# One-hot rows of a graph layer built from pairs of 16-bit numbers, in groups of blocks on VectorE

## The chip, the cores and the metric

The kernel runs on one core of a Trainium2 chip. The core has five engines that run side by side and are tied together by semaphores only: PE (TensorE, matmul and transpose, results in PSUM), DVE (VectorE), ACT (ScalarE), POOL (GpSimd) and SP (SyncE, which mainly issues DMAs). The metric is the device time of one execution in microseconds. Before the change it is 753.4 us, the median of three runs (752.56 to 754.88).

## The reference, cut to what matters

There are 1250 nodes with 512 features and 21250 edges (20000 random ones and one loop per node), sorted by target. Two layers follow each other, each on a layer-normalised and rectified input, each added to `x`:

```python
h = max(layernorm(x), 0)
# graph attention
h = h @ W + b_w
e = leaky_relu((h @ a[:512])[dst] + (h @ a[512:])[src] + b_a, 0.2)
w = exp(e)
x += segment_sum(w / segment_sum(w, dst)[dst] * h[src], dst)
# mixture of four experts, each of two graph convolutions; each node uses its best two
h = max(layernorm(x), 0)
gates = softmax(h @ gate_W + gate_b);  top_v, top_i = top_k(gates, 2)
conv(h) = relu(segment_mean(h[src], dst) @ Wl + bl + h @ Wr)
x += sum over the two chosen experts of top_v * conv2(conv1(h))
```

## The kernel before, in words

The edges are turned into a dense matrix of counts, `AT[source, target]`, and both layers use it as a matrix. Nodes lie in `NT` = 10 tiles of `T` = 125, and edges in `NB` = 170 blocks of `EB` = 125, one edge of a block per partition. As the edges are sorted by target, the targets of tile `t` lie in a window of 19 to 23 neighbouring blocks (`window[t]`), and successive windows share about six blocks.

**How the counts arise.** The count matrix of a tile is a sum of matmuls over the blocks of its window: a one-hot row per edge for its target (`hd`) times a one-hot row per edge for its source (`hs`). To count all 1250 sources with one row of 125, the source number is written as `q * 125 + low`. The row has its one at `low`, and the one is replaced by the power of two `4 ** q` (`val`). The sum in PSUM is thus a packed number, of which two bits hold the count for each of the ten source tiles. One more column of ones, at `T`, gives the degree of the target. The packed sum is copied out (`pack`, `deg`), transposed (L374), and its ten digits are cut out by shifts and masks (`digit`, L356 and L359) and cast to `AT` (L421).

`hd` is made by one VectorE comparison per tile (L382): `iota` (16-bit floats, 0 to 1252) against `idx["dst"]` (32-bit floats, one number per edge and block, repeated along 128 columns). `hs` is made block by block into a ring of `RING` = 27 rows in the tile `first`, because the windows overlap and a row can be used by two tiles. Three blocks in four are made by one VectorE instruction (L399: equal to `low`, then times `val`, both as numbers per partition). Each fourth block is made by two ScalarE instructions (L394, L395): the distance from `low`, and `relu(val - val * distance)`. `low`, `val` and `less` (minus `val`) are computed once for all blocks (L304 to L310).

**The stages in order.** First x, W and the indices are loaded, the indices are transposed so that a block's edges lie on partitions (L284), and copied to `idx` (L286). The vector `a` is spread over partitions and W is multiplied with it (L294), so that the projection also gives both attention scores. `project(t)` normalises a tile of x (L178, ScalarE), transposes it (L185), rectifies it into `hT` (L186), multiplies it by W (L333) and adds the bias on VectorE (L335). The statistics that `normalize` needs are made by `norms` in batches: for tiles 0 and 1, for 2 to 4, and for 5 to 9, the last batch when `project(5)` starts. A batch is a bn_stats (L168) and a bn_aggr (L169) per tile, then one square root on ScalarE (L171), one reciprocal (L172) and one product (L174) for all its tiles.

The target tiles form three chunks (tiles 0-3, 4-6 and 7-9). `count(ci)` counts one chunk, `attend(ci)` does its attention: scores on ScalarE (L435, L436), times counts on VectorE (L442), matmul with `hW` on PE (L448), sum of the weights on POOL (L446). `count(0)` is woven into the projections of tiles 2 to 7, `count(1)` into `attend(0)`, and `count(2)` into `attend(1)`. Then come the second normalisation (L491 makes the gate sums), the means over neighbours (L578), and the four experts (from about 235 us on, L854 to L1036), which work on the chosen nodes gathered into slots. `number_slots`, among the means, numbers the slots of each expert: its VectorE comparison L734 makes a one-hot row of 128 for each node, expert and tile (`spots`).

**What sets the order.** The text gives each engine's instructions an order and a priority, but the planner of the tile framework may issue a ready instruction ahead of ones written earlier, so the order in the trace differs from the text: source rows that `count(0)` writes after the second projection stand among the preparations at 15 us. `tc.keep_in_program_order(i)` holds instruction `i` behind the instruction of the same engine that was written last before it. Each engine then runs its queue strictly in order. The pool `hot` has two buffers per tile (`hd`, `xn`, `hT`, `pack`), the pool `small` three, and PSUM eight banks.

## Time and profile before

| | before |
|---|---|
| median of 3 runs | 753.4 us (752.56 to 754.88) |
| the profiled execution | 752.97 us, of which 751.2 us is the span |
| PE busy | 715.0 us (95%) |
| PE weight loads | 580.0 us (77%) |
| DVE busy | 500.0 us (67%) |
| ACT busy | 247.3 us (33%) |
| POOL busy | 164.6 us (22%) |
| mean granted PE clock | 0.987 |

The span is the time from the first to the last instruction. "Busy" is the time in which an engine has at least one instruction under way; the ends of matmuls are modelled, so a busy PE need not be at its peak. A line of the timeline or of the groups names an engine, a line of the code, the operation, and the tiles as output<-input. In brackets or behind a bar stands how long the engine was idle just before, and whose result ended the idle time. A share of busy time over the whole span says little here, since the stages have different limits: the experts take two thirds of the span, and the changed lines all lie in the first third.

### The profile page before, as it was taken

Reading aid. Unit: us, or ns where it says so; the run is one execution under the profiler, and the core shown is the slowest. Engines: PE = TensorE matmul, PEld = TensorE weight load, DVE = VectorE, ACT = ScalarE, POOL = GpSimd, SP = SyncE. Lnnn points to the kernel's source line nnn. Section 1 sums busy time; section 2 is a strip of 40 time slices with the busy share of each in tenths; the row PEclk is TensorE's granted clock in tenths of the full one; section 3 lists DMA queues with packets and bytes.
Section 4 is the critical chain, followed back from the end, with each engine's and each line's share of the span. In section 5 each row is a group of like instructions: output and inputs, shape, how many; then the busy total and the mean of one; then the engine's idle time right before and its main releaser. Section 6 shows DMA issues by size and latency. Waiting matters only on the chain. (4 is left out here: it accounts for less than half of the span.)

```text
span 751.2 us, 9943 instructions
## 1 busy us (share of the span) xinstructions
PE 715.0 (95%) x3409; PEld 580.0 (77%) x3409; DVE 500.0 (67%) x1321; ACT 247.3 (33%) x565; POOL 164.6 (22%) x151
## 2 busy tenths in 40 slices
PE   7969999998999999899999999999999999999993
PEld 4757545545998888788888888888888888887883
DVE  6898899699887569356964554568364554557642
ACT  4648957872200012111222333103031333104320
POOL 1101544231002002020132321300232321400431
PEclk9989999999999999999999999999999999999997
DMA  8000001101307312181133223721132322601332
GB/s 213 8 8 4 4 8 58 43 7 42 118 23 188 119 55 72 44 283 42 56 99 56 35 47 57 228 97 44 54 80 47 49 38 51 186 28 57 81 64 30
DMA packets 30636, 52.95 MB, mean 70 GB/s; under 512 B 7305, under 2 KB 8755, under 8 KB 30568
## 3 DMA queue, kind: packets, MB, share of 16 engines
q0 software_dynamic: 6848, 15.77, 11.3%
q1 hardware_dynamic: 15570, 20.44, 9.2%
q10 hardware_dynamic: 8150, 15.90, 6.2%
q8 instruction: 34, 0.56, 0.3%
q14 instruction: 34, 0.28, 0.1%
HBM read 33.55 MB, written 19.20 MB: 70 GB/s over the span
## 5 line engine op out<-in xcount | busy, mean ns | idle before, releaser
L448 PE MATMUL p_o<-hW,P 125*125 125x512 f32 x200 | 91.4, 598 | 1.8 <-DVE P L442 1.6
L960 PE MATMUL p_s<-h_hi,AS 125*128 125x512 f32 x210 | 83.8, 399 | 1.1 <-DVE v L932 1.1
L117 ACT ACTIVATE h_hi<-v 125x512 fp32r<-125x512 f32 x40 | 24.9, 629 | 178.8 <-DVE v L929 141.2
L960 PE MATMUL p_s<-h_lo,AS 125*128 125x512 f32 x210 | 81.8, 389 | 0.0
L864 PE MATMUL p<-T,S 128*125 128x256 f32 x320 | 73.9, 382 | 0.4 <-DVE v L913 0.2
L864 PEld LDWEIGHTS p<-T,S 128*125 128x125 f32 x320 | 60.3, 189 | 11.0 <-DVE v L913 2.0
L966 DVE TENSOR_SCALAR agg<-p_s,asel 128x512 f32<-128x512 f32 x22 | 16.5, 750 | 76.2 <-PE p_f L854 39.4
L841 ACT CAST AS<-digs 125x256 fp32r<-125x256 int32 x150 | 54.8, 403 | 36.9 <-DVE digs L356 31.4
L846 POOL DMA_INDIRECT hsel<-h,reads x32 | 36.3, 1136 | 133.2 <-DMA h<-v 54.0
L448 PEld LDWEIGHTS p_o<-hW,P 125*125 125x125 f32 x200 | 35.3, 188 | 37.4 <-issue 34.6
L972 POOL DMA_INDIRECT out_dram<-y,writes x22 | 35.4, 1608 | 130.9 <-ACT y L1008 59.0
L446 POOL TENSOR_TENSOR den<-den,P 125x375 f32<-125x375 f32 (+1 forms) x27 | 40.2, 1490 | 46.5 <-DVE P L442 42.1
L356 DVE TENSOR_SCALAR digs<-packed 125x128 int32<-125x128 int32 x279 | 45.6, 219 | 3.0 <-ACT packed L835 2.2
L960 PEld LDWEIGHTS p_s<-h_hi,AS 125*128 125x128 f32 x210 | 39.4, 188 | 9.6 <-issue 1.4
L856 ACT ACTIVATE gT<-p_f 128x512 f32<-128x512 f32 x22 | 13.5, 616 | 99.8 <-PE p_f L854 99.8
L960 PEld LDWEIGHTS p_s<-h_lo,AS 125*128 125x128 f32 x210 | 39.5, 188 | 8.0
L827 POOL DMA_INDIRECT asel<-packs,reads x35 | 36.5, 1043 | 33.2 <-DVE agg L966 19.4
L333 PE MATMUL p_h<-W_sb,hT 128*125 128x257 f32 (+1 forms) x160 | 40.6, 408 | 2.9 <-ACT hT L186 2.8
L578 PE MATMUL p_ag<-AT,h_hi 125*128 125x416 f32 (+1 forms) x120 | 42.6, 355 | 0.0
L864 PE MATMUL p<-wr,h2T 128*125 128x256 f32 x160 | 39.3, 390 | 3.4 <-DVEq L1071 2.3
L578 PE MATMUL p_ag<-AT,h_lo 125*128 125x416 f32 (+1 forms) x120 | 42.2, 352 | 0.0
L399 DVE TENSOR_SCALAR first<-iota,low,val 125x125 bf16<-125x125 f16 x128 | 39.4, 378 | 1.9 <-PE p_a L403 1.9
(239 smaller groups left out, 1443.5 us busy)
## 6 DMA issues: line engine op xcount, KB each, us to landing
h<-v SPq DMA_DIRECT2D x40, 224.0 KB
wl<-in_L_gnn_Wl_dram ACTq DMA_DIRECT2D x7, 1024.0 KB
wr<-in_L_gnn_Wr_dram ACTq DMA_DIRECT2D x7, 1024.0 KB
out_dram<-x SPq DMA_DIRECT2D x10, 224.0 KB
x<-in_x_dram SPq DMA_DIRECT2D x1, 1120.0 KB
h<-v SPq DMA_DIRECT2D x40, 26.0 KB
W_sb<-in_L_gnn_W_dram SPq DMA_DIRECT2D x4, 256.0 KB
wl<-in_L_gnn_Wl_dram SPq DMA_DIRECT2D x1, 1024.0 KB
```

Of the source, the lines that this page charges most:

```text
L333: nc.tensor.matmul(p[:T, :n], hT[:, k, :], W_sb[:, k, half, :n], start=(k == 0), stop=(k == KF - 1))
L356: nc.vector.tensor_scalar(o, v, BITS * d, (1 << BITS) - 1, op0=OP.logical_shift_right, op1=OP.bitwise_and)
L399: nc.vector.tensor_scalar(hs[:, :T], iota[:EB, :T], low[:, j:j + 1], val[:, j:j + 1], op0=OP.is_equal, op1=OP.mult)
L446: nc.gpsimd.tensor_add(den[:, :n], den[:, :n], P[:, :n])
L448: nc.tensor.matmul(po[i][:T, :], P[:, i * T:(i + 1) * T], hW[:, s - 1, :, :HD], start=(s == 1), stop=(s == NT))
L578: nc.tensor.matmul(p[:, :n], h2[s][i][:, m * 128:(m + 1) * 128], AT[:, s, c], start=(s == 0 and i == 0), stop=(s == NT - 1 and i == 1))
L827: nc.gpsimd.indirect_dma_start(a, None, packs, bass.IndirectOffsetOnAxis(reads[:, j:j + 1], 0))
L841: nc.scalar.copy(AS[:, d:d + 2, :], dig)
L846: nc.gpsimd.indirect_dma_start(r, None, h1, bass.IndirectOffsetOnAxis(reads[:, j:j + 1], 0))
L864: nc.tensor.matmul(p, A[:, k, :], B[:, k, :], start=(i == 0 and k == 0), stop=(i * KF + k == n - 1))
L960: nc.tensor.matmul(p, A[:, s, :], hs[s][f], start=(s == order[0] and f == 0), stop=(s == order[-1] and f == 1))
L972: s = nc.gpsimd.indirect_dma_start(out, bass.IndirectOffsetOnAxis(writes[:, j:j + 1], 0), y, None, bounds_check=N - 1, oob_is_err=False, c ...
```

## The change

The diff does five things.

1. **Targets.** `idx["dst"]` becomes a 16-bit float with every number written twice (`twice`), and the comparison for `hd` views 128 columns as 64 pairs (`by_two`): the repeated operand now has two equal adjacent 16-bit numbers in its innermost dimension, where it had one 32-bit number with a step of zero.
2. **Sources.** `low` (16-bit float) and `val` (bfloat16) are also written twice. `source_rows` makes up to eight blocks at once by two VectorE instructions: a comparison with `low` into the ring and a multiplication by `val` in place. A group ends where the ring or the tile's window ends. The two ScalarE instructions per fourth block, `far` and `less` are gone. A row is `HOT` = 126 wide, the column of ones stands at 126, and the ring's rows are 128 numbers apart instead of 126.
3. **Preparation.** The power of two is made in `power`, and copied to the bfloat16 pairs. `idx["src"]` and `power` live in the pool that is released after the first projection.
4. **Statistics.** The batch for tiles 5 to 9 is written right after the first `hd` (`next(counts0)`) instead of at the start of `project(5)`, and each of its bn_aggr is held in program order.
5. **Spots.** The comparison of L734 works on pairs as well, from a 16-bit copy of `at` with every number twice.

The diff, without the context that says nothing more:

```diff
@@ -158,7 +158,7 @@
     AT = adj.tile([T, NT, N], F32R, name="AT")
     AT32 = AT.bitcast(F32)
-    def norms(tiles):
+    def norms(tiles, in_order=False):
         n = len(tiles)
@@ -166,7 +166,9 @@
         for i, xt in enumerate(tiles):
             st = small.tile([T, 6], F32, name="st")
             nc.vector.bn_stats(st, xt)
-            nc.vector.bn_aggr(mv[:, i, :], st)
+            last = nc.vector.bn_aggr(mv[:, i, :], st)
+            if in_order:
+                tc.keep_in_program_order(last)
         rs = small.tile([T, NT], F32, name="rs")
         nc.scalar.activation(rs[:, :n], mv[:, :n, 1], AF.Sqrt, bias=eps[:T, :])
         nc.vector.reciprocal(rs[:, :n], rs[:, :n])
@@ -225,9 +227,10 @@
     load_x(5, NT)
     first = feat.tile([128, KF * N], F32, name="first", tag="first")
-    SW = T + 1
+    HOT = T + 1
+    SW = HOT + 1
     RING = max(hi - lo + 1 for lo, hi in window) + 4
-    spare = first[:, RING * SW // 2:]
+    spare = first[:, RING * 64:]
     a_line = spare[:1, :2 * D]
     nc.scalar.dma_start(a_line, rows_of(a, 1, 2 * D))
@@ -243,8 +246,8 @@
     iota = build.tile([128, NI], F16, name="iota")
     nc.gpsimd.iota(iota, pattern=[[1, NI]], base=0, channel_multiplier=0,
                    allow_small_or_imprecise_dtypes=True)
-    ring = first[:, :RING * SW // 2].bitcast(BF16).rearrange("p (r n) -> p r n", r=RING)
-    nc.gpsimd.memset(ring[:, :, T:], 1.0)
+    ring = first[:, :RING * 64].bitcast(BF16).rearrange("p (r n) -> p r n", r=RING)
+    nc.gpsimd.memset(ring[:, :, HOT:], 1.0)
@@ -274,6 +277,13 @@
     a_b = [spread(a_line[:, h * D:(h + 1) * D], D) for h in range(2)]
+    def twice(name, dtype):
+        return build.tile([EB, NB, 2], dtype, name=name)
+    def by_two(v):
+        return v.rearrange("p r (a b) -> p r a b", b=2)
     idx = {}
     for name in ("dst", "src"):
@@ -282,9 +292,14 @@
         p = bank("p_i")
         for c in range(2):
             nc.tensor.transpose(p[:EB, c * NH:(c + 1) * NH], f[:, c, :], ident[:NH, :NH])
-        i = build.tile([EB, NB], F32, name=f"i_{name}")
-        nc.scalar.copy(i.rearrange("p (j c) -> p c j", c=2),
-                       p[:EB, :NB].rearrange("p (c j) -> p c j", c=2))
+        pv = p[:EB, :NB].rearrange("p (c j) -> p c j", c=2)
+        if name == "dst":
+            i = twice("i_dst", F16)
+            nc.scalar.copy(i.rearrange("p (j c) b -> p c j b", c=2),
+                           pv[:, :, :, None].to_broadcast([EB, 2, NH, 2]))
+        else:
+            i = prep.tile([EB, NB], F32, name="i_src")
+            nc.scalar.copy(i.rearrange("p (j c) -> p c j", c=2), pv)
         idx[name] = i
     xnorms = norms(xs[:2])
@@ -296,18 +311,17 @@
                 op0=OP.mult, op1=OP.mult, accum_out=W_sb[:, k, half, HD:]))
     xnorms += norms(xs[2:5])
-    low = build.tile([EB, NB], F32, name="low")
-    val = build.tile([EB, NB], I32, name="val")
-    less = build.tile([EB, NB], F32, name="less")
+    low, val = twice("low", F16), twice("val", BF16)
+    power = prep.tile([EB, NB], I32, name="power")
     q = prep.tile([EB, NB], F32, name="q")
     shift = 0.5 - 0.5 / T
     nc.vector.tensor_scalar(q, idx["src"], 1.0 / T, -shift, op0=OP.mult, op1=OP.add)
     nc.vector.tensor_scalar(q, q, ROUND, -ROUND, op0=OP.add, op1=OP.add)
-    nc.vector.scalar_tensor_tensor(low, q, float(-T), idx["src"], op0=OP.mult, op1=OP.add)
-    nc.vector.tensor_scalar(val, q, float(BITS), 127.0, op0=OP.mult, op1=OP.add)
-    nc.vector.tensor_scalar(val, val, 23, None, op0=OP.logical_shift_left)
-    val = val.bitcast(F32)
-    nc.vector.tensor_scalar(less, val, -1.0, None, op0=OP.mult)
+    nc.vector.scalar_tensor_tensor(low, q[:, :, None].to_broadcast([EB, NB, 2]), float(-T),
+                                   idx["src"][:, :, None].to_broadcast([EB, NB, 2]), op0=OP.mult, op1=OP.add)
+    nc.vector.tensor_scalar(power, q, float(BITS), 127.0, op0=OP.mult, op1=OP.add)
+    nc.vector.tensor_scalar(power, power, 23, None, op0=OP.logical_shift_left)
+    nc.vector.tensor_copy(val, power.bitcast(F32)[:, :, None].to_broadcast([EB, NB, 2]))
     for half in range(2):
         junk = prep.tile([128, 2, HD], F32, name="junk")
         nc.vector.scalar_tensor_tensor(junk, bw_b[:, :, :HD], 1.0,
@@ -318,8 +332,6 @@
     def project(t):
-        if t == 5:
-            xnorms.extend(norms(xs[5:NT]))
         xn = hot.tile([T, D], F32, name="xn")
         normalize(xn, xs[t], xnorms[t])
         hT = hot.tile([128, KF, T], F32, name="hT")
@@ -358,7 +370,20 @@
         else:
             nc.vector.tensor_scalar(o, v, BITS * d, None, op0=OP.logical_shift_right)
-    made = set()
+    made = [0]
+    GROUP = 8
+    def source_rows(until):
+        while made[0] < until:
+            j0 = made[0]
+            j1 = min(j0 + GROUP, until, (j0 // RING + 1) * RING)
+            made[0] = j1
+            n = [EB, j1 - j0, HOT // 2, 2]
+            hs = by_two(ring[:EB, j0 % RING:(j1 - 1) % RING + 1, :HOT])
+            nc.vector.tensor_tensor(hs, by_two(iota[:EB, None, :HOT]).to_broadcast(n),
+                                    low[:, j0:j1, None, :].to_broadcast(n), op=OP.is_equal)
+            nc.vector.tensor_tensor(hs, hs, val[:, j0:j1, None, :].to_broadcast(n), op=OP.mult)
     def count(ci):
@@ -379,28 +404,19 @@
             lo, hi = window[t]
             nb = hi - lo + 1
             hd = hot.tile([EB, RING - 4, 128], BF16, name="hd")
+            pairs = [EB, nb, 64, 2]
             rows = nc.vector.tensor_tensor(
-                hd[:, :nb, :], iota[:EB, None, t * T:t * T + 128].to_broadcast([EB, nb, 128]),
-                idx["dst"][:, lo:hi + 1, None].to_broadcast([EB, nb, 128]), op=OP.is_equal)
+                by_two(hd[:, :nb, :]), by_two(iota[:EB, None, t * T:t * T + 128]).to_broadcast(pairs),
+                idx["dst"][:, lo:hi + 1, None, :].to_broadcast(pairs), op=OP.is_equal)
             if t == 0:
                 tc.keep_in_program_order(rows)
             yield
             p = bank("p_a")
             for j in range(lo, hi + 1):
-                hs = ring[:EB, j % RING, :]
-                if j not in made and j % 4 == 3:
-                    far = hot.tile([EB, T], BF16, name="far")
-                    nc.scalar.activation(far, iota[:EB, :T], AF.Abs, bias=low[:, j:j + 1], scale=-1.0)
-                    nc.scalar.activation(hs[:, :T], far, AF.Relu, bias=val[:, j:j + 1],
-                                         scale=less[:, j:j + 1])
-                    made.add(j)
-                elif j not in made:
-                    nc.vector.tensor_scalar(hs[:, :T], iota[:EB, :T], low[:, j:j + 1],
-                                            val[:, j:j + 1], op0=OP.is_equal, op1=OP.mult)
-                    made.add(j)
-                i = nc.tensor.matmul(p[:, :SW], hd[:, j - lo, :], hs, start=(j == lo), stop=(j == hi))
+                if j >= made[0]:
+                    source_rows(min(j + GROUP, hi + 1))
+                i = nc.tensor.matmul(p[:, :SW], hd[:, j - lo, :], ring[:EB, j % RING, :SW], start=(j == lo), stop=(j == hi))
                 if t == 0 and j == lo:
                     tc.keep_in_program_order(i)
                 if (j - lo) % 4 == 3 and j < hi:
@@ -408,7 +424,7 @@
                     turn()
             pack = hot.tile([T, T], F32, name="pack")
             nc.scalar.copy(pack, p[:T, :T])
-            nc.scalar.copy(deg[:, t:t + 1], p[:T, T:T + 1])
+            nc.scalar.copy(deg[:, t:t + 1], p[:T, HOT:SW])
             store(packs[t * T:(t + 1) * T, :T], pack)
             counted.append((t, pack))
             yield
@@ -518,6 +534,7 @@
     next(third)
     counts0 = count(0)
     next(counts0)
+    xnorms += norms(xs[5:], in_order=True)
     n = steps(0) - ND // 2 - 1
     weave(in_turn(third, *(project(t) for t in range(3, NT - 2))), 2 * NT - 9, islice(counts0, n), n)
     pieces = [attend(ci) for ci in range(3)]
@@ -729,10 +746,13 @@
             nc.vector.tensor_copy(told[:, :, f], left)
             if f + 1 < FLD:
                 nc.vector.tensor_sub(left, left, told[:, :, f])
+        at2 = book.tile([T, NE * NT, 2], F16, name="at2")
+        nc.vector.tensor_copy(at2, at[:, :, None].to_broadcast([T, NE * NT, 2]))
         for e in range(NE):
             c = slice(e * NT, (e + 1) * NT)
-            nc.vector.tensor_tensor(spots[:, c, :], steps_h[:, None, :].to_broadcast([T, NT, SLOTS]),
-                                    at[:, c, None].to_broadcast([T, NT, SLOTS]), op=OP.is_equal)
+            pairs = [T, NT, SLOTS // 2, 2]
+            nc.vector.tensor_tensor(by_two(spots[:, c, :]), by_two(steps_h[:, None, :]).to_broadcast(pairs),
+                                    at2[:, c, None, :].to_broadcast(pairs), op=OP.is_equal)
         mine = mix_tiles[0][0].rearrange("p k n -> p (k n)").bitcast(BF16)[:T, :NE * NT * NS].rearrange(
             "p (c q) -> p c q", q=NS)
```

## The prediction

> **What bounds the kernel now.** I read the chain of waits first. It begins only at 378.3 us, inside the expert layers, and the changed operations lie ahead of 235 us, so it can't price them. Next I cut the span into stages. Columns: window, length, then busy time (and instructions) of PE, PE weight loads, VectorE (DVE), ScalarE (ACT) and GpSimd (POOL), granted PE clock, DMA share, GB/s.
>
> ```profile
> 0.00:75.00 75.00, 61.59 (x316) 47.26 (x317) 62.55 (x172) 45.43 (x107) 8.96 (x26) 0.95 0.24 58
> 75.00:135.00 60.00, 58.90 (x248) 29.22 (x247) 55.20 (x107) 45.94 (x106) 28.42 (x19) 1.00 0.08 22
> 135.00:200.00 65.00, 61.35 (x267) 41.05 (x267) 57.62 (x150) 36.91 (x71) 12.13 (x11) 1.00 0.10 27
> ```
>
> From 75 to 135 us PE has 1.1 us of idle: the attention matmuls (L448) run end to end there (8 in 3.65 us), and faster rows find nothing to shorten. Only the first 75 us have idle PE time, 13.4 us. The same columns in slices of 4 us show where:
>
> ```profile
> 36.00:40.00 4.00, 3.03 (x21) 2.48 (x20) 3.71 (x10) 1.19 (x3) 0.21 (x1) 1.00 0.00 0
> 40.00:44.00 4.00, 0.21 (x1) 0.00 (x0) 4.00 (x8) 0.51 (x3) 0.00 (x0) 0.78 0.06 16
> 44.00:48.00 4.00, 2.91 (x13) 2.40 (x14) 4.00 (x15) 3.35 (x6) 0.00 (x0) 0.50 0.00 0
> 48.00:52.00 4.00, 4.00 (x23) 3.38 (x22) 3.81 (x8) 1.01 (x4) 0.00 (x0) 0.86 0.00 0
> ```
>
> PE does next to nothing for 4 us while VectorE is full, and then its granted clock drops to 0.50. The timeline of PE, then of VectorE (start, us, line, operation, instructions, idle before and its releaser):
>
> ```profile
> 40.64 0.21 PE L403 MATMUL p_a<-first,hd 125*128 125x126 bf16 x1 [1.61 <-DVE first L399]
> 45.05 1.09 PE L185 MATMUL p_t<-ident,xn 125*128 125x125 f32 x4 [4.19 <-ACT xn L178]
> 46.82 4.84 PE L333 MATMUL p_h<-W_sb,hT 128*125 128x257 f32 x16
> 53.54 3.73 PE L333 MATMUL p_h<-W_sb,hT 128*125 128x257 f32 x16 [0.37 <-ACT hT L186]
> ...
> 35.89 0.69 DVE L168 BATCH_NORM_STATS2 st<-x 125x6 f32<-125x512 f32 x1
> 40.59 3.19 DVE L382 TENSOR_TENSOR hd<-iota,i_dst 125x2944 bf16<-125x2944 f16 x1
> 43.70 0.18 DVE L172 RECIPROCAL rs<-rs 125x5 f32<-125x5 f32 x1
> 44.06 2.78 DVE L399 TENSOR_SCALAR first<-iota,low,val 125x125 bf16<-125x125 f16 x12
> ```
>
> The statistics of the last five tiles of x run from 35.9 to 40.6 us. While they run the count's next source row is late (the 1.61), and the reciprocal that ends them sits behind a 3.19 us one-hot of targets, so `xn` of tile 5 and its transposes are late (the 4.19). The clock after the gap makes 16 projection matmuls take 4.84 us against 3.73 later, the four transposes 1.09 against 0.59, six count matmuls 0.83 against 0.50: 1.9 us in all. Gap plus clock is 7.7 us.
>
> The groups that the change touches (columns: busy, mean ns, idle before):
>
> ```profile
> L399 DVE TENSOR_SCALAR first<-iota,low,val 125x125 bf16<-125x125 f16 x128 | 39.4, 378 | 1.9 <-PE p_a L403 1.9
> L395 ACT ACTIVATE first<-far,val,less 125x125 bf16<-125x125 bf16 x42 | 19.6, 487 | 12.0 <-PE p_a L403 10.4 <-DVE less L310 1.6
> L382 DVE TENSOR_TENSOR hd<-iota,i_dst 125x2944 bf16<-125x2944 f16 x6 | 19.3, 3210 | 0.0
> L382 DVE TENSOR_TENSOR hd<-iota,i_dst 125x2432 bf16<-125x2432 f16 x2 | 5.4, 2682 | 0.0
> L394 ACT ACTIVATE far<-iota,low 125x125 bf16<-125x125 f16 x42 | 15.6, 394 | 1.7 <-DVE low L306 1.4
> L734 DVE TENSOR_TENSOR x<-steps_h,at 125x1280 bf16<-125x1280 f16 x4 | 5.8, 1473 | 0.0
> L741 DVE TENSOR_TENSOR x<-T,told 125x2200 bf16<-125x2200 bf16 x1 | 2.4, 2428 | 0.0
> ```
>
> **The change part by part.** *Rate of the new comparisons.* The two shapes of L382 give (3210 - 2682) / 512 = 1.03 ns per element and 170 ns fixed. No two-source row of before does better; L741, all 16-bit but with a step of 0 innermost, takes 1.1. A rate of two per cycle does exist for one source: the digits (L356, 500 int32) follow each other every 0.35 us, 0.7 ns per element with the fixed part in it. So the new form costs between 1.03 and half, 0.52 ns per element. I take the half: what L382 and L734 lack is a 16-bit second operand with adjacent elements, and the pairs supply just that.
>
> [...]
>
> *Targets (L382), ten instructions.* 2944, 2816 and 2432 elements become 1.69, 1.63 and 1.43 us: 16.3 against 30.9 in all (19.3 + 6.2 + 5.4). In the first four tiles 6.4 against 12.2. Bounds: 30.9 (no gain) and 16.3.
>
> *Sources.* 128 VectorE instructions (39.4 us) and 84 ScalarE ones (15.6 + 19.6 = 35.2 us) go. In come 32 groups of up to eight blocks (three or four per tile, one more where a group meets the end of the ring), each a compare and an in-place multiply. Eight blocks are 1008 elements: 0.69 us each, 1.41 with 0.03 between dependent instructions (as between L457 and L458). For 170 blocks: 2 x (21420 x 0.52 + 32 x 170) = 33 us; at the slow end 55. The first four tiles hold 71 blocks, 12 groups: 13.4 or 22.5 us; the 69 old instructions of the first 75 us took 16.7.
>
> *Sum of VectorE:* 49 against 70 us, 21 less; at the slow end 86, 16 more. ScalarE loses 35 us and gains 0.15 (the i_dst copy writes 340 numbers, not 170; 500 elements took 0.58 at L186). Nearly all of it lies under PE and is worth nothing by itself; what counts is the first 63 us.
>
> *Stage from 23.2 us (PE starts tile 2) to 62.9 us (last count of the first chunk), 39.7 us long.* PE work in it is 33.0 busy less 1.9 of slow clock = 31.1. VectorE then has 6.4 targets + 13.4 sources + 5 for the sums at L335 (12 of 0.41) + 3.9 statistics (five of 0.66 + 0.09, and the tail) = 28.7. PE is the longer, by 2.4 us only.
>
> *Statistics earlier.* Five bn_stats, five bn_aggr, one Sqrt on ScalarE, one reciprocal and one product move from 35.9-44.2 us. The pin holds each bn_aggr behind the VectorE instruction written last before it, its own bn_stats, which it needs anyhow; it is the earlier place in the text that moves them. Source rows written later still were issued from 14.98 us on, so I expect the statistics between 19 us (x has landed: DMA share 0.26 at 19-20, 0.09 after) and 29. They issue no DMA and pass nothing on SP's or POOL's queue. Behind them in VectorE's queue wait the L335 sums of tile 2 (eight PSUM banks, so PE goes on) and the first source groups. Removed: 4.2 + 1.6 of gap, 1.9 of clock. Late next is the first group of tile 0, if it is made behind the statistics: 1.41 before its first matmul against 0.31. I charge 1.4; bounds 0 (it fits VectorE's 1.38 us gap at 18.8) and 4 (PE waits out the whole block of statistics, or VectorE waits from 15.5 to 19.5 us for x).
>
> *New waits.* A group overwrites slots 27 blocks back and waits for the last count matmul on any of them; behind it in VectorE's queue stand the L335 sums and the next hd. Its slots are those of the preceding tile's first blocks, four to twelve matmuls ahead, under 1 us of PE. Bounds 0 and 1.1 for each of nine later groups of the first chunk, 10 us; I take 0, nearest to L399's 1.9 us of idle in 128 instructions.
>
> *Preparation before 15 us.* `low` and `val` of 340 numbers in place of 170, a cast more and `less` gone: 0.33 + 0.24 + 0.24 becomes near 0.5 + 0.24 + 0.4: 0.3 us, bounds 0 and 0.4. Against it, ScalarE no longer makes rows at 17.6-19.9 us, ahead of the Sqrt of tiles 2 to 4 at 19.87; PE waits 1.1 us for that between 21.4 and 23.2. I count 0.5, bounds 0 and 1.1.
>
> *Spots (L734)* go from 5.8 to 3.3 us plus a 0.2 copy, between 200 and 235 us, where PE is 19.9 of 20 us busy on means: 0. Without that cover it would be 2.3 us either way at most.
>
> *Count matmuls* of 127 columns for 126: 220 at under 1 ns, dropped.
>
> Sum: -4.2 - 1.6 - 1.9 - 0.5 + 0.3 + 1.4 = -6.5 us, against the profiled execution's 752.97 us (span 751.2 and 1.8 around it; median of the runs 753.4, so 0.4 above it): 746.5.
>
> **Rivals.** *B, group waits take the gap's place.* VectorE is within 2.4 us of PE in the stage, and matmuls that had waited for one row of 0.23 us wait for two instructions of a group. For it: L395's 10.4 us of waits on p_a show rows made just behind the matmuls. Against: blocks can be made up to four beyond the window. With half of the twelve groups exposed by 1.1 us, 6.6 us come back: 753.1, no change (749 to 754).
>
> *C, slower: the comparisons stay at one element per cycle.* In the stage VectorE would have 12.2 + 22.5 + 5 + 3.9 = 43.6 us in place of 39.7 elapsed: +3.9, or +2.3 if 1.6 us of it fits VectorE's gaps ahead of 23.2. From 75 to 135 us six tiles' sources would take 2 x (99 x 126 x 1.03 + 20 x 170) = 32.5 us against 39.4 - 16.7 = 22.7, that is 65 in a stage of 60: +5. Together 760 (756 to 763). It decides where the rate is above some 0.9 ns per element (stage full at 39.7). For it: every two-source row shown, L741 above all. Against: L741 has no adjacent pair, the new operands do.
>
> *D, more than forecast.* No first-group wait, the 1.1 at 21-23 us wholly gone, and the 1.1 us of PE at 133.7 (p_x behind `deg`, queued on a busy ScalarE) as well: -4.2 - 1.6 - 1.9 - 1.1 - 1.1 = -9.9: 743.
>
> **How the numbers follow.** A 0.59 (743.5 to 750), B 0.15, C 0.14, D 0.12. What a measurement can tell from no change is 0.3%, 2.3 us: 751.1 to 755.7. Slower: C and a little of B, 0.17. Same: most of B, 0.09. Faster: A, D and the rest of B, 0.74. The range leaves out half of D below and most of C above: 742 to 756.
>
> **What would show it.** Right: L382's successor at 1.4-1.7 us in all ten tiles, odd ones too; compare and multiply at about 0.7 us for eight blocks; the last five bn_stats by 30 us; PE without a wait over 1.5 us between 24 and 63 us, clock 1.00 there; the first L448 near 65.7 us, not 72.2; every later stage as long as before. Wrong: hd at 3 us (C); PE waiting for `first` several times a tile (B); or the expert stage getting longer, which nothing here prices.

## The result, and the profile after

The changed kernel takes 740.25 us (median of 6 runs, 738.92 to 740.85). Six runs of the kernel before have a median of 754.71 us (752.56 to 755.60). The ratio is 0.9816, with a 95% interval of 0.9803 to 0.983: 14.5 us less, where 6.5 had been forecast. The forecast of "faster" was right; 740.25 lies below the forecast range of 742 to 756.

| | before | after |
|---|---|---|
| profiled execution | 752.97 us | 738.92 us |
| span | 751.2 us | 737.1 us |
| PE busy | 715.0 us (95%) | 709.9 us (96%) |
| DVE busy | 500.0 us (67%) | 483.2 us (66%) |
| ACT busy | 247.3 us (33%) | 219.0 us (30%) |
| mean granted PE clock | 0.987 | 0.996 |

**Where the time went.** I cut the span at events that both kernels have: the first attention matmul (`p_o`), the first matmul of the means over neighbours (`p_ag`), the first and last `p_s` and the last `p_y` of the experts. Each column is the mean of two profiled executions (of before and its repetition, and of after and its repetition):

| stretch | before | after | difference |
|---|---|---|---|
| start to first `p_o` | 72.7 | 63.0 | -9.7 |
| first `p_o` to first `p_ag` (attention) | 106.2 | 104.8 | -1.5 |
| to first `p_s` | 120.1 | 119.7 | -0.4 |
| first to last `p_s` (experts) | 427.0 | 426.0 | -1.0 |
| last `p_s` to last `p_y` | 14.1 | 14.1 | 0 |
| last `p_y` to the end | 12.5 | 10.7 | -1.9 |

The sum is -14.5 us, the measured gain. Two thirds lie where they were looked for, ahead of 63 us, but they are 9.7 us and not 6.5. The experts' 1.0 can't be called an effect of the change: two profiles of one kernel differ there by 1.5 us (before) and 1.8 us (after).

The stages of the changed kernel, in the columns of the prediction's first fence; the last line is the stage from PE's start on tile 2 to the first `p_o`:

```profile
0.00:75.00 75.00, 67.98 (x357) 50.43 (x358) 60.50 (x143) 37.44 (x75) 13.93 (x29) 1.00 0.24 58
75.00:135.00 60.00, 60.00 (x260) 31.08 (x259) 47.21 (x92) 34.05 (x74) 22.38 (x17) 1.00 0.10 24
135.00:200.00 65.00, 61.33 (x275) 45.38 (x274) 57.88 (x171) 28.40 (x52) 10.81 (x9) 1.00 0.19 65
22.10:62.80 40.70, 38.95 (x258) 33.17 (x258) 35.38 (x77) 17.36 (x37) 4.30 (x10) 1.00 0.03 7
```

The same stage of the kernel before, from its windows:

```profile
23.19:72.20 49.01, 42.21 (x257) 34.92 (x258) 45.29 (x108) 30.03 (x72) 4.11 (x9) 0.93 0.03 6
```

The stage is 8.3 us shorter. PE's idle time in it falls from 6.80 us (49.01 less 42.21) to 1.75, and PE's busy time by 3.26 at a clock of 1.00 instead of 0.93. VectorE's busy time falls by 9.9 us. This one line of before already holds the point that the prediction missed: VectorE was busy for 45.3 us of 49.0, more than PE with its 42.2.

The prediction's own stage is shorter: from tile 2 to the last count of the first chunk. Its windows, before and then after:

```profile
23.20:62.90 39.70, 33.02 (x207) 27.05 (x208) 37.26 (x93) 20.79 (x54) 3.63 (x6) 0.91 0.02 6
22.10:53.93 31.83, 30.08 (x208) 25.38 (x209) 28.20 (x61) 8.76 (x21) 3.76 (x8) 1.00 0.03 7
```

What PE still waits for from tile 2 to the first `p_o`, from its timeline after the change (start, us, line, operation, idle before and its releaser):

```profile
25.67 0.61 PE L419 MATMUL p_a<-first,hd 125*128 125x127 bf16 x8
...
26.55 0.61 PE L419 MATMUL p_a<-first,hd 125*128 125x127 bf16 x8
...
31.80 0.23 PE L419 MATMUL p_a<-first,hd 125*128 125x127 bf16 x1 [0.68 <-DVE hd L408]
...
33.36 0.37 PE L399 MATMUL p_x<-ident,pack 125*125 125x125 f32 x1 [0.47 <-ACT deg L427]
```

The 4.19 us and the 1.61 us are gone; 0.68 and 0.47 are left. The first counts of tile 0 no longer go matmul by matmul but eight in a row (0.61 us). In the kernel before, seven took 1.11 us, at a granted clock of 1.00 from 27.6 to 28.8 us:

```profile
27.67 1.11 PE L403 MATMUL p_a<-first,hd 125*128 125x126 bf16 x7
```

VectorE writes a row every 0.23 us there (ten in 2.32), and most of the seven matmuls (215 ns each) start just as the one before ends, so that waiting for single rows hardly shows as idle time. VectorE after the change, at the same time:

```profile
23.04 1.42 DVE L408 TENSOR_TENSOR hd<-iota,i_dst 125x2432 bf16<-125x2432 f16 x1
24.37 1.28 DVE L168 BATCH_NORM_STATS2 st<-x 125x6 f32<-125x512 f32 x2
...
28.48 0.19 DVE L174 RECIPROCAL rs<-rs 125x5 f32<-125x5 f32 x1
...
30.11 1.64 DVE L408 TENSOR_TENSOR hd<-iota,i_dst 125x2816 bf16<-125x2816 f16 x1
```

The statistics stand at 24.4 to 28.1 us, where before they stood at 35.9 to 40.6. And the groups that the change made, among them the targets (L408), the sources (L384, L386) and the spots (L754), over the first 230 us (busy, mean ns, idle before):

```profile
L384 DVE TENSOR_TENSOR first<-iota,low 125x1008 bf16<-125x1008 f16 x15 | 13.0, 873 | 0.4 <-PE p_a L419 0.4
L386 DVE TENSOR_TENSOR first<-first,val 125x1008 bf16<-125x1008 bf16 x15 | 11.3, 760 | 0.1
L408 DVE TENSOR_TENSOR hd<-iota,i_dst 125x2944 bf16<-125x2944 f16 x6 | 10.2, 1697 | 0.1
...
L408 DVE TENSOR_TENSOR hd<-iota,i_dst 125x2816 bf16<-125x2816 f16 x2 | 3.3, 1634 | 0.8 <-PE p_a L419 0.8
L754 DVE TENSOR_TENSOR x<-steps_h,at 125x1280 bf16<-125x1280 f16 x4 | 3.0, 820 | 0.0
L408 DVE TENSOR_TENSOR hd<-iota,i_dst 125x2432 bf16<-125x2432 f16 x2 | 2.8, 1424 | 0.0
...
L761 DVE TENSOR_TENSOR x<-T,told 125x2200 bf16<-125x2200 bf16 x1 | 2.4, 2441 | 0.0
```

The targets take 16.3 us in all (10.2 + 3.3 + 2.8), as forecast. L384 and L386 in all their shapes keep VectorE busy for 37.2 us: the sources cost it nearly as much as the 39.4 of the old form, which ScalarE's 35.2 helped besides. The spots fall by 2.8.

PE's waits from the first `p_o` to 200 us, after (waiter, releaser, us in total, times, longest):

```profile
PE p_t L187 <- ACT h L180: 2.0, 1, 2.0
PE p_o L464 <- DVE P L458: 1.6, 1, 1.6
```

Before, the same view has one line more, `p_x` behind ScalarE's `deg`, 1.1 us: most of the 1.5 that the attention gained.

### The profile page after: what moved, and what is told of

Read it like the earlier page. It is cut to its first block, busy times and chain, and to the rows that moved or that the text cites. A ratio compares the mean times of both kernels' runs of the same rounds, so it can differ in the third digit from the quotient of the medians.

```text
span 737.1 us, 9775 instructions
## 1 busy us (share of the span) xinstructions
PE 709.9 (96%) x3409; PEld 577.5 (78%) x3409; DVE 483.2 (66%) x1258; ACT 219.0 (30%) x481; POOL 162.6 (22%) x151
## 4 chain that ended last, share of the span: by engine, by line
PE 50%; issue 4%; POOL 2%; DMA 1%; DVE 1%; POOLq 0%; ACT 0%; another core or an unknown queue 0%; SPq 0%; DVEq 0%
PE p L884 23%; PE p_y L884 14%; PE p_s L980 10%; PE p_f L874 2%; POOL out_dram L992 1%; POOL asel L847 1%; DMA hsel<-h,reads 1%; POOL hsel L866 1%; PE p_as L853 0%; DMA h<-v 0%; DVE wl L964 0%; DVE h_lo L120 0%; DVE y L1036 0%; DVE agg L986 0%; ACT h_hi L117 0%
## 5 line engine op out<-in xcount | busy, mean ns | idle before, releaser
L884 PEld LDWEIGHTS p<-T,S 128*125 128x125 f32 x320 | 59.8, 188 | 10.5 <-DVE v L933 1.6
L992 POOL DMA_INDIRECT out_dram<-y,writes x22 | 35.4, 1609 | 130.0 <-ACT y L1028 58.1
L462 POOL TENSOR_TENSOR den<-den,P 125x375 f32<-125x375 f32 (+1 forms) x27 | 37.3, 1381 | 50.1 <-DVE P L458 46.9
L368 DVE TENSOR_SCALAR digs<-packed 125x128 int32<-125x128 int32 x279 | 45.6, 220 | 3.0 <-ACT packed L855 2.2
L980 PEld LDWEIGHTS p_s<-h_hi,AS 125*128 125x128 f32 x210 | 39.4, 188 | 9.6 <-issue 1.4
L876 ACT ACTIVATE gT<-p_f 128x512 f32<-128x512 f32 x22 | 13.5, 616 | 100.0 <-PE p_f L874 99.8
L595 PE MATMUL p_ag<-AT,h_lo 125*128 125x416 f32 (+1 forms) x120 | 42.2, 352 | 0.0
L884 PE MATMUL p<-wl,S 128*125 128x256 f32 x160 | 38.4, 379 | 0.1
```

Source lines behind the costliest of these rows:

```text
L368: nc.vector.tensor_scalar(o, v, BITS * d, (1 << BITS) - 1, op0=OP.logical_shift_right, op1=OP.bitwise_and)
L462: nc.gpsimd.tensor_add(den[:, :n], den[:, :n], P[:, :n])
L595: nc.tensor.matmul(p[:, :n], h2[s][i][:, m * 128:(m + 1) * 128], AT[:, s, c], start=(s == 0 and i == 0), stop=(s == NT - 1 and i == 1))
L884: nc.tensor.matmul(p, A[:, k, :], B[:, k, :], start=(i == 0 and k == 0), stop=(i * KF + k == n - 1))
L980: nc.tensor.matmul(p, A[:, s, :], hs[s][f], start=(s == order[0] and f == 0), stop=(s == order[-1] and f == 1))
L992: s = nc.gpsimd.indirect_dma_start(out, bass.IndirectOffsetOnAxis(writes[:, j:j + 1], 0), y, None, bounds_check=N - 1, oob_is_err=False, c ...
```

## The experiments

Two explanations fit this profile alike. By the prediction's, the gap at 41 to 45 us comes from where the last statistics stand, so that writing them earlier removes it. By the other, VectorE has too much to do in the whole stage, and whatever is last in its queue when PE needs it shows as the gap; then the halved comparisons remove it. The expectations give the theories letters, and in the later ones L is the theory that the stage's length follows VectorE's work.

Times are medians; "ratio" is against the kernel before on the same chip, with its 95% interval. The stage in the table runs from PE's start on tile 2 to the first `p_o`; PE, DVE and ACT are busy us in it, attention is the time from the first `p_o` to the first `p_ag`.

| run | us | ratio | stage | PE | DVE | ACT | clock | attention |
|---|---|---|---|---|---|---|---|---|
| before | 754.7 | 1 | 49.0 | 42.2 | 45.3 | 30.0 | 0.93 | 106.2 |
| e2_stats_only | 756.9 | 1.0036 (1.002 to 1.0052) | 49.3 | 42.3 | 45.6 | 31.6 | 0.93 | 108.1 |
| e3_pairs_only | 741.5 | 0.9833 (0.9803 to 0.9863) | 41.2 | 39.0 | 35.0 | 17.3 | 1.00 | 104.8 |
| e4_wide | 770.1 | 1.0212 (1.018 to 1.0243) | 54.5 | 44.8 | 50.4 | 18.7 | 0.91 | 116.4 |
| e5_targets | 747.8 | 0.9932 (0.9911 to 0.9954) | 42.2 | 39.3 | 37.8 | 30.1 | 1.00 | 104.9 |
| e6_sources | 746.2 | 0.9914 (0.9892 to 0.9935) | 46.4 | 40.8 | 44.1 | 19.5 | 0.96 | 105.4 |
| e7_act_back | 742.7 | 0.9866 (0.985 to 0.9883) | 41.1 | 38.9 | 36.2 | 36.9 | 1.00 | 104.7 |
| e8_no_act | 757.9 | 1.0071 (1.0044 to 1.0099) | 51.3 | 43.2 | 48.7 | 17.8 | 0.90 | 110.5 |
| e10_group4 | 743.6 | 0.9842 (0.9815 to 0.987) | 43.4 | 40.5 | 37.6 | 17.5 | 0.96 | 104.8 |
| e11_group16 | 741.5 | 0.9824 (0.9785 to 0.9863) | 40.5 | 38.9 | 34.6 | 17.5 | 1.00 | 104.8 |
| e12_old_spots | 742.7 | 0.9841 (0.9807 to 0.9876) | 40.7 | 38.9 | 35.2 | 17.3 | 1.00 | 104.8 |
| after | 740.25 | 0.9816 (0.9803 to 0.983) | 40.7 | 38.9 | 35.4 | 17.4 | 1.00 | 104.8 |

**e1_control: the kernel before, once more**

> The kernel before, once more, for the part of the gain that lies outside the changed stages. In the two profiles the time from the first slot matmul (L753, 227.8 and 216.9 us) to the end shrank from 523.4 to 520.2 us, and the first matmul started at 2.5 instead of 3.4 us. Theory chance: these 4 us come from the landing of the first DMA and from the granted clock after a wait, and differ from one execution to the next; then this profile shows another value, off by 1 us or more from 523.4. Theory cause: the change shortens the expert layers; then this profile shows 523.4 within 0.5 us and the first matmul at 3.4.

Measured: 754.18 us, ratio 1.0001 (0.9983 to 1.0018), with the gap of 4.19 us in the same place. Differences of 0.3% can be told. From the first slot matmul to the end this profile has 525.5 us, 2.1 more than the first one of the same kernel, and its first matmul starts at 2.4 us, not 3.4: differences of this size there are chance.

**e2_stats_only: the earlier statistics alone**

```diff
     def project(t):
-        if t == 5:
-            xnorms.extend(norms(xs[5:NT]))
...
     next(counts0)
+    xnorms += norms(xs[5:], in_order=True)
```

> Of the change only the statistics move: the batch for tiles 5 to 9 is written behind the first hd, rows are made as before. Theory A (both parts are needed): the gap of 4.2 us and its slow clock go, but VectorE has 12.2 + 16.7 + 5 + 3.9 = 37.8 us of work in a stage of which PE has 31.1, so most of it comes back as waits of the count matmuls: the first attention matmul 2 to 4 us earlier than 72.2, the time 750 to 752 us. Theory B (the place of the statistics is the whole gain): first attention matmul near 63 us, the time 741 to 744 us.

Measured: 756.88 us, 0.36% slower. Both expectations missed: the step that had been credited with the whole gain gives none. PE's timeline of this kernel says why:

```profile
28.75 2.87 PE L333 MATMUL p_h<-W_sb,hT 128*125 128x257 f32 x12 [1.01 <-ACT hT L188]
...
37.18 0.60 PE L403 MATMUL p_a<-first,hd 125*128 125x126 bf16 x4 [2.78 <-DVE hd L382]
...
39.67 5.40 PE L333 MATMUL p_h<-W_sb,hT 128*125 128x257 f32 x16
...
72.53 3.35 PE L448 MATMUL p_o<-hW,P 125*125 125x512 f32 x5 [1.85 <-DVE P L442]
```

The wait for `xn` is gone, as planned. In its place PE waits 2.78 us for the next one-hot of targets at 37.2, which VectorE issues at 34.0 instead; then the clock falls all the same (sixteen projection matmuls in 5.40 us, where 3.73 is usual at 1.00), and before 72.5 the first attention matmuls wait 1.85 us for `P`. VectorE has as much to do as before, 45.6 us, and the stage is as long as before, 49.3. Behind the wait for `P` the clock falls once more (0.98 over the stretch from 75 to 135 us, where the kernel before has 1.00): the first eight attention matmuls take 5.40 us where the kernel before needs 3.67. That is nearly all of the 1.9 us by which attention is longer.

**e3_pairs_only: all but the earlier statistics**

```diff
     def project(t):
+        if t == 5:
+            xnorms.extend(norms(xs[5:NT]))
...
     next(counts0)
-    xnorms += norms(xs[5:], in_order=True)
```

> The change without the move of the statistics: their batch is written at the start of the fifth projection again. Theory A: VectorE is freed of 10 us in the stage, so it comes to the statistics earlier and they stand behind an hd of 1.7 us, not 3.2; a gap of 1 to 3 us stays: first attention matmul at 64 to 67 us, the time 742 to 746 us. Theory B (the place of the statistics is the whole gain): a gap of 4 us and slow clock as before, the time 750 to 753 us.

Measured: 741.49 us, a little better than theory A; the interval of its ratio contains that of the changed kernel. From its windows and its PE timeline:

```profile
22.30:63.50 41.20, 39.03 (x258) 33.41 (x258) 35.03 (x75) 17.35 (x37) 3.94 (x10) 1.00 0.03 7
```

```profile
37.93 0.27 PE L421 MATMUL p_a<-first,hd 125*128 125x127 bf16 x2 [0.91 <-DVE first L388]
38.85 0.65 PE L187 MATMUL p_t<-ident,xn 125*128 125x125 f32 x4 [0.66 <-ACT xn L180]
...
40.25 3.73 PE L347 MATMUL p_h<-W_sb,hT 128*125 128x257 f32 x16
```

The statistics are written where the kernel before writes them, and the two waits of that place, on `first` and on `xn`, are 0.91 and 0.66 us instead of 1.61 and 4.19. The sixteen projections behind them run at a granted clock of 1.00 (3.73). So the gap was VectorE's arrears. The place of the statistics in its queue decided only which tile was late.

**e4_wide: grouped and written twice, but in 32 bits**

```diff
-            i = twice("i_dst", F16)
+            i = twice("i_dst", F32)
...
-    low, val = twice("low", F16), twice("val", BF16)
+    low, val = twice("low", F32), twice("val", F32)
```

> The changed kernel with the pairs (targets, low, val) as 32-bit floats: the same instructions in nearly the same order, but no operand pair of 16 bits. Theory rate: hd of 23 blocks takes 3.2 us again, eight source rows 1.2 us per instruction, VectorE has 43.6 us of work in the first chunk's stage and bounds it: first attention matmul at 68 to 72 us, and 65 us of VectorE work from there to 135, the time 750 to 760 us. Rival (grouping and the freed ScalarE give the gain, the rate is hidden under PE): first attention matmul at 63 to 65 us, the time 740 to 743 us.

Measured: 770.08 us, 2% slower than before and above both forecasts; hd at 3.2 us came as the theory of the rate has it. The groups of this kernel over the first 200 us:

```profile
L386 DVE TENSOR_TENSOR first<-first,val 125x1008 bf16<-125x1008 bf16 x15 | 20.3, 1351 | 0.1
L408 DVE TENSOR_TENSOR hd<-iota,i_dst 125x2944 bf16<-125x2944 f16 x6 | 19.3, 3216 | 0.0
L384 DVE TENSOR_TENSOR first<-iota,low 125x1008 bf16<-125x1008 f16 x15 | 18.7, 1268 | 0.0
```

The types shown are those of the first operand; the second is 32 bits wide here. That alone takes the comparison of targets back from 1.70 to 3.22 us, where the old form takes 3.21. The pairs without the 16 bits are worth nothing, and the rate is worth some 30 us against the changed kernel. PE's waits from 77 to 200 us in this kernel:

```profile
PE p_x L399 <- ACT deg L427: 7.2, 4, 4.2
```

Here attention suffers as well, with the groups at 2.6 us a pair of instructions: it takes 116.4 us, 10 more than before. VectorE is busy for 108.6 of them (before: 95.1 of 106.2). PE loses 7.2 us to these waits, and its busy time grows by 5.3 at a clock of 0.96. In the kernel before ScalarE made a quarter of the rows; without that help and without the rate VectorE holds back two stages. For attention this is read from its busy time and was not tested by itself.

**e5_targets and e6_sources: one comparison each in the new form**

e5 is the kernel before with the pairs for targets alone; sources, statistics and spots stay as they were. e6 is the changed kernel with the old comparison of targets.

```diff
 e5, against before
+            i = twice("i_dst", F16)
...
-                hd[:, :nb, :], iota[:EB, None, t * T:t * T + 128].to_broadcast([EB, nb, 128]),
-                idx["dst"][:, lo:hi + 1, None].to_broadcast([EB, nb, 128]), op=OP.is_equal)
+                by_two(hd[:, :nb, :]), by_two(iota[:EB, None, t * T:t * T + 128]).to_broadcast(pairs),
+                idx["dst"][:, lo:hi + 1, None, :].to_broadcast(pairs), op=OP.is_equal)
```

```diff
 e6, against after
-            i = twice("i_dst", F16)
+            i = build.tile([EB, NB], F32, name="i_dst")
...
-                by_two(hd[:, :nb, :]), by_two(iota[:EB, None, t * T:t * T + 128]).to_broadcast(pairs),
-                idx["dst"][:, lo:hi + 1, None, :].to_broadcast(pairs), op=OP.is_equal)
+                hd[:, :nb, :], iota[:EB, None, t * T:t * T + 128].to_broadcast([EB, nb, 128]),
+                idx["dst"][:, lo:hi + 1, None].to_broadcast([EB, nb, 128]), op=OP.is_equal)
```

> Of the change only the targets: hd by pairs, source rows and statistics as before. Theory L (what counts is VectorE's work until the first attention matmul, wherever it stands): hd saves 8.9 us there (six of them) and 5.8 in the first chunk; the run with the pairs alone took 13 us off the time by saving about 9 us of VectorE and 13 of ScalarE in the stage, so this one gets about half: first attention matmul at 66 to 69 us, the time 745 to 749 us. Rival S (ScalarE's share of the rows was the brake): little, 750 to 754 us.

> The changed kernel with the old targets (hd at 3.2 us); sources by pairs in groups, ScalarE freed, statistics early. Theory L: VectorE has 12.2 + 13.4 + 5 + 3.9 = 34.5 us in the stage, 5.8 more than with the change and 3.4 more than PE's 31.1: first attention matmul at 65 to 69 us, the time 743 to 749 us. Rival S: the freed ScalarE gives most, 740 to 742 us.

Measured: 747.83 and 746.20 us, 5.1 and 6.7 us less than the 752.93 before; both lie in their forecast. e5 does the most for the first stage (42.2 us, VectorE 37.8): of VectorE's time in the stage the changed kernel saves 8.7 us by targets (18.6 to 9.9) and only 2.9 by sources (15.1 to 12.2). PE in e5 still waits for the statistics, 2.60 us instead of 4.19, and this wait leaves the clock at 1.00:

```profile
41.57 0.65 PE L185 MATMUL p_t<-ident,xn 125*128 125x125 f32 x4 [2.60 <-ACT xn L178]
...
42.89 3.73 PE L346 MATMUL p_h<-W_sb,hT 128*125 128x257 f32 x16
```

e6 still has 44.1 us of VectorE work and a stage of 46.4. Its PE timeline shows the late targets:

```profile
33.07 0.23 PE L414 MATMUL p_a<-first,hd 125*128 125x127 bf16 x1 [2.38 <-DVE hd L403]
...
67.69 0.67 PE L459 MATMUL p_o<-hW,P 125*125 125x512 f32 x1 [1.76 <-DVE P L453]
```

Together the two gains are 11.8 us, against 13.5 to 14.5 for the whole: neither part makes the other needless. e6 gains in other places too: its stage starts earlier (21.3 us, against 24.0 in e5), and its last stretch, from the last `p_y` to the end, is 10.8 us against 12.1.

**e7_act_back and e8_no_act: what ScalarE's relief is worth**

e7 is the changed kernel with two ScalarE instructions again for every fourth block; their results are used by nothing. e8 is the kernel before with every source row made on VectorE.

```diff
 e7, against after, in source_rows
+            for j in range(j0, j1):
+                if j % 4 == 3:
+                    far = hot.tile([EB, T], BF16, name="far")
+                    nc.scalar.activation(far, iota[:EB, :T], AF.Abs, bias=eps[:EB, :], scale=-1.0)
+                    waste = hot.tile([EB, T], BF16, name="waste")
+                    nc.scalar.activation(waste, far, AF.Relu, bias=eps[:EB, :], scale=eps[:EB, :])
```

```diff
 e8, against before, in count
-                if j not in made and j % 4 == 3:
+                if False:
```

> The changed kernel with ScalarE's old load put back: for each fourth block two activations of 125x125 (about 35 us in all) whose results nobody uses. Theory L: ScalarE is no bound, it costs the 1.1 us wait of p_x for deg near 134 us and 0.5 to 1.1 us at 21 to 23 us: 741 to 743 us. Rival S: the time goes back by half of the gain or more, 746 us and up.

> The kernel before with every source row made on VectorE in the old form, one instruction per block; ScalarE makes none. Theory L: VectorE gets 42 instructions of 0.23 to 0.39 us more, 4 us of them in the first stage and 8 from 75 to 135 us where it is busy for 55 of 60 us: 756 to 764 us. Rival S: relief of ScalarE outweighs it, 745 to 752 us.

Measured: 742.67 and 757.90 us, both in the forecast of theory L. e7's stage is 41.1 us although ScalarE is busy for 36.9 of them, more than the 30.0 before. Its ratio lies 0.5% above that of the changed kernel and its median 2.4 us. In the profiles the difference is 2.8 us: 1.0 ahead of the stage, 0.5 in it, and 1.6 among the means, where the slowest matmul of `p_ag` with `h_lo` takes 553 ns and in the changed kernel 360. That isn't ScalarE's doing: in e11, without its rows, the slowest takes 552, and in the kernel before, with them, 360. So ScalarE's relief is a small part of the gain, and two thirds of that part lie ahead of the stage. PE starts tile 2 at 23.1 to 24.0 us (mean 23.4) in the five profiles in which ScalarE makes rows (before, e1, e2, e5, e7), and at 21.3 to 23.3 us (mean 22.3) in the other nine; the two ranges overlap. e8, with 48.7 us of VectorE work in the stage, is slower than before by 5.0 us. Its stage starts early too, at 21.5 us, and takes 51.3, so the first `p_o` is no later than before; the loss lies in attention, which takes 110.5 us and in which PE waits 2.9 us for `deg` and is busy for 2.1 us more at a clock of 0.98. VectorE is busy for 100.3 us there, ScalarE for 65.9 instead of 77.9. So in the old form ScalarE's share was worth having there.

**e9_after_again: the changed kernel, beside the next three**

> The changed kernel once more, for the three us that it gained behind 178 us. So far the time from the first to the last p_s matmul was 426.1 and 427.5 us in two profiles of the kernel before, 424.9 with the change, 428.6 with the pairs alone; from the last p_s matmul to the end 26.5, 27.2, 24.9 and 24.7. Theory chance: the first number falls anywhere between 424.5 and 429 here. Theory cause: it is 424.9 within 0.5. The second number is 24.5 to 25.2 if the change shortens the end, 26 to 27.5 if that was chance. First attention matmul at 62.8 within 0.7, the time 739 to 742 us.

Measured: 741.14 us, ratio 0.9814 (0.9789 to 0.984), first `p_o` at 63.2 us. From the first to the last `p_s` it takes 426.95 us, so what the first profile gained in the experts was chance. From the last `p_s` to the end it takes 24.8, so the shorter end belongs to the change.

**e10_group4 and e11_group16: the size of a group**

```diff
-    GROUP = 8
+    GROUP = 4      (e10)
+    GROUP = 16     (e11)
```

> Groups of four blocks instead of eight: the fixed 170 ns are paid for some 50 groups instead of 32, 2 x 18 x 0.17 = 6 us more of VectorE work, 2.5 of it in the first stage, where VectorE would have 31.2 against PE's 31.1; the first count matmul of a group waits 0.9 instead of 1.41. Theory L: 741 to 744 us. Rival (waiting for whole groups is what is left of waits): 738 to 740 us.

> Groups of up to sixteen blocks: some 24 groups instead of 32, 2 x 8 x 0.17 = 2.7 us less of VectorE work, 1.1 of it in the first stage, and a group takes 2.5 us before its first matmul. Theory L: VectorE has slack in the stage already, so 0 to 1 us better, or as much worse by the longer wait of the first group: 739.5 to 742 us.

Measured: 743.63 us, ratio 0.9842 (0.9815 to 0.987), and 741.49 us, ratio 0.9824 (0.9785 to 0.9863). Both lie in the forecast of theory L. Groups of four cost VectorE 37.6 us in the stage instead of 35.4, and the stage takes 43.4 at a clock of 0.96, 2.7 us more: PE waits for the second `hd`, and behind this wait of 1.89 us, shorter than e5's 2.60, the clock falls (sixteen projection matmuls in 4.76 us).

```profile
33.44 0.23 PE L419 MATMUL p_a<-first,hd 125*128 125x127 bf16 x1 [1.89 <-DVE hd L408]
...
35.63 4.76 PE L345 MATMUL p_h<-W_sb,hT 128*125 128x257 f32 x16
```

Groups of sixteen can't be told from eight. The prediction had feared for such groups that PE waits out two long instructions (its rival B); even sixteen blocks at a time give a stage of 40.5 us.

**e12_old_spots: the spots compared in the old form**

```diff
-            nc.vector.tensor_tensor(by_two(spots[:, c, :]), by_two(steps_h[:, None, :]).to_broadcast(pairs),
-                                    at2[:, c, None, :].to_broadcast(pairs), op=OP.is_equal)
+            nc.vector.tensor_tensor(spots[:, c, :], steps_h[:, None, :].to_broadcast([T, NT, SLOTS]),
+                                    at[:, c, None].to_broadcast([T, NT, SLOTS]), op=OP.is_equal)
```

> The changed kernel with the spots made in the old way (1.47 us each, four of them, no 16-bit copy): 2.4 us more of VectorE work between 190 and 220 us, under the matmuls of the means. Theory: no difference that can be measured, 739 to 742 us. Rival: the slots are numbered later and the first expert's gathers with them, 742 to 744 us.

Measured: 742.67 us, ratio 0.9841 (0.9807 to 0.9876), which overlaps with the changed kernel's. The median lies in the rival's range, but mostly for another reason: the first `p_o` comes 1.2 us later (64.0 against 62.8), since PE starts tile 2 at 23.3 us instead of 22.1, where the spots have no part. Of the rival itself the profiles show a little. From the experts' first matmul `p` to the first `p_as`, which takes the gathered rows, it is 60.88 us in all six profiles with the old spots and 60.51 or 60.52 in all eight with the new ones. The spots are thus worth 0.4 us, the third row of the table of stretches, and too little for the run times to tell.

## Why the prediction was right or wrong

**Right: the rate.** Half the old time per element for the pairs, (1697 - 1424) / 512 = 0.53 ns against 1.03, in all ten tiles: 1.70, 1.63 and 1.42 us against the 1.69, 1.63 and 1.43 forecast. The odd tiles, whose `iota` slice begins at byte 250, 750 and so on, no multiple of four, run at the same rate. No row of the kernel before has two sources at this rate. That the pairs would reach it was the author's estimate, and the runs showed it: 0.53 ns with pairs of 16 bits, and no gain with pairs of 32 (3.22 us for 23 blocks, e4). For one source the trace of before has the half: L356 takes 415 ns for 500 numbers (the eight in the stage) and 219 for 128, (415 - 219) / 372 = 0.53 ns each. The prediction's "cycle" stands for the 1.03 ns of one element in L382; no run shows a clock of VectorE. Two instructions for eight blocks take 0.675 and 0.677 us in the first 65 us, 0.69 forecast. The one-hot L761, all 16-bit but with a step of 0 innermost, stays at 2.44 us (2.43 before).

**Right: VectorE and PE as they would be after.** In the prediction's stage they are busy for 28.2 and 30.1 us, against 28.7 and 31.1. The statistics stand between 19 and 29 us, and PE waits for no group. The new waits are 0.68 + 0.47 us against the 1.4 charged, but that they come near it is luck: the 1.4 was for the first group of tile 0, where PE has no wait, and these two are for the second `hd` and a `deg`.

**Wrong: the step "Statistics earlier", "Removed: 4.2 + 1.6 of gap, 1.9 of clock".** The 7.7 us do go, but not by that step. e2 makes it alone and gains nothing (756.9 us); e3 leaves it out and gains nearly all (741.5), and e5 gains 5.1 us by the lighter targets alone. The prediction read the last item of VectorE's queue as the cause (the reciprocal, whose input ScalarE had ready at 41.0 us, started at 43.7 behind the 3.19 us of `hd`), where the queue as a whole was behind. Of VectorE's lighter work it said that nearly all "lies under PE and is worth nothing by itself; what counts is the first 63 us", and for these it set VectorE against PE only as they would be after the change. The same stage of the kernel before, with VectorE busy for 37.3 of 39.7 us against PE's 33.0, would have named VectorE as the bound, and the comparisons as the part that carries the gain. The clock term is right in size, but a matter of chance as well: behind the wait of 4.19 us the clock fell in both profiles of the kernel before (0.93 over the stage in each), behind e5's 2.60 it did not (1.00), and behind e10's 1.89 it did (0.96).

**Wrong: the sizes.** Against the sum of -6.5:

- *First stage, -9.7.* PE's idle time from 23 us on falls by 5.05 us, against -4.4 forecast (-5.8 + 1.4). PE's busy time falls by 3.26, against 1.9. The count matmuls alone go from 8.46 to 6.83 us, where the prediction had taken 0.33 of slow clock, and the rest is not the clock: the 81 of 87 that ran at 1.00 already took 7.62 us in the kernel before. They started one by one as their rows came, so short waits counted as busy time. e5, which still makes source rows one by one but on a VectorE with less to do, needs 6.88 for all 87, so it isn't the groups that save this. And the stage starts 1.1 us earlier (22.10 against 23.19) where 0.5 - 0.3 = 0.2 had been counted. The means over the profiles (23.4 and 22.3) suggest that ScalarE without rows to make is worth more there than the 0.5 taken, near its bound of 1.1. The first `p_o` comes at 62.8 us, not near 65.7.
- *Attention, -1.5.* The wait of `p_x` for `deg`, 1.1 us, went: it was the whole idle time between 75 and 135 us, in which the prediction saw nothing to shorten. Only rival D had it, as a matter of ScalarE's queue. ("Only the first 75 us have idle PE time" also passes over 3.65 us between 135 and 200, in the prediction's own row; they stayed, 3.67 after.) e5 and e7 lose the wait too, with ScalarE as busy as before or busier; what these two share with the changed kernel is the lighter VectorE.
- *The end, -1.9.* Nothing priced it. The last stretch is 10.5 to 10.8 us in all eight profiles with grouped 16-bit sources, 11.9 to 12.9 in the other six, e4 among these. Most of it is one place: from GpSimd's last branch to its next instruction it is 0.52 us in the eight and 1.77 to 1.95 in the six. Why the change alters that stays open.
- *The spots, -0.4.* They had been put at 0; e12 shows the 0.4.

**The rivals.** D, more than forecast (743), came nearest: its two terms of 1.1 us came, one in attention and one ahead of the stage, though the first not through ScalarE's queue. PE had no wait at the first group, as D has it, but 1.15 us of others. B did not occur, even with e11's long groups. Nor did C; e4 makes its case and shows that it was priced too low, 770 instead of 760. Attention grew by 10 us instead of 5, and the first `p_o` came 4.4 us later than before instead of 2.3 to 3.9.

## What to carry to other kernels

When an engine waits for one late item, add up all the work of the engine that makes it, over the whole stage: if that sum is near the stage's length (45 of 49 us here, more than PE's 42), moving the item only makes the next one late (e2), while less work helps (e3, e5). The larger of the two sums is a floor: in all the profiles here the stage was 1.6 to 4.2 us longer than it (PE's 39 us and VectorE's 35 gave 40.7). And PE's sum was itself too high while it waited (42.2 us before, 38.9 after), by the clock (0.93) and by waits too short to show. A comparison with a repeated operand took half the time per element (0.53 against 1.03 ns) once that operand was stored twice, 16 bits wide, so that pairs are adjacent; in 32 bits the same form gained nothing (e4, 3.22 us against 3.21).

## What the runs showed of the hardware that was not expected

The granted clock after a wait differed between executions of equal instructions. In the experts, PE waits 2.35 us in the kernel before and 2.39 us in the changed one at the same place; the matmuls that follow are slow in the first only (the first eight take 3.14 us, in the second 1.96). When the changed kernel ran again (e9), they were slow too (2.81). From PE's timeline before:

```profile
318.11 3.14 PE L864 MATMUL p<-wr,h2T 128*125 128x256 f32 x8 [2.35 <-DVEq L1071]
...
321.05 4.17 PE L864 MATMUL p<-T,S 128*125 128x256 f32 x16
```

after:

```profile
306.85 1.96 PE L884 MATMUL p<-wr,h2T 128*125 128x256 f32 x8 [2.39 <-DVEq L1091]
...
308.65 3.62 PE L884 MATMUL p<-T,S 128*125 128x256 f32 x16
```

and in e9:

```profile
307.48 2.81 PE L884 MATMUL p<-wr,h2T 128*125 128x256 f32 x8 [2.55 <-PEq L1091]
...
310.08 4.50 PE L884 MATMUL p<-T,S 128*125 128x256 f32 x16
```

That is 1.7 us on work that the change doesn't touch, and a reason not to read differences of 1 to 2 us in the experts as effects. From 20 us to the last matmul the granted clock of the kernel before is 1.00 but for two stretches at 0.50: from 42.3 to 49.1 us, which begins in the wait of 4.19 us, and from 318.7 to 322.2 us, which begins 0.6 us behind the wait of 2.35. The changed kernel's first profile has 1.00 throughout. Its four waits of more than 1 us (1.62, 2.04, 2.39 and 1.05) all left the clock at 1.00, as did five of the seven before (1.61, 1.10, 1.61, 2.03 and 1.07).

The new instructions take longer in attention than ahead of it: a comparison of eight blocks takes 0.675 us on the mean up to 65 us, and 0.873 over all fifteen of the first 230 us. From VectorE's timeline after, just behind the first `p_o`:

```profile
66.71 1.54 DVE L384 TENSOR_TENSOR first<-iota,low 125x1008 bf16<-125x1008 f16 x1 [0.40 <-PE p_a L419]
...
68.29 0.68 DVE L386 TENSOR_TENSOR first<-first,val 125x1008 bf16<-125x1008 bf16 x1
```

and from POOL's:

```profile
66.46 1.25 POOL L462 TENSOR_TENSOR den<-den,P 125x500 f32<-125x500 f32 x1 [2.92 <-DVE P L458]
```

The slow comparison runs beside POOL's sum of the weights, the product 0.04 us behind it runs alone at the usual 0.68. Of the thirty such instructions four take 1.54 to 1.73 us, each beside 1.0 us or more of POOL's sums; the 21 with no sum beside them take 0.66 to 0.68. But so does the comparison at 106.4 us, which started before POOL's sum and overlaps with it for 0.45 us. That the two engines hinder each other was not shown. These long instructions are why the sources cost VectorE 37.2 us and not the 33 forecast: 88 blocks take 14.6 us up to 65 us, the other 82 take 22.5. No loss by it shows, since PE is never idle from 75 to 135 us.
